# Selective scan: the last two convolution blocks on TensorE beside the scan's first steps

## The chip, the cores and the metric

The kernel runs on one core of a Trainium2 chip. TensorE (PE) multiplies matrices into PSUM, VectorE (DVE), ScalarE (ACT) and GpSimd (POOL) work element by element, and SyncE (SP) starts the transfers. Each engine works through its own instructions in order and waits on semaphores for the others. The metric is the time of one execution on the device in microseconds (us), as the median of several runs. The profile is one further execution, recorded by the hardware profiler.

## The reference

A batch of 8 images, 64 x 64 positions (L = 4096) with 96 channels, goes through four layers, each with a group norm ahead of it and a residual sum behind it. Layers 0 and 2 are selective-scan blocks, layer 1 is a chunked scan and layer 3 an up- and downsampling with a small network between. The change concerns layers 0 and 2. Such a layer does this, for 192 inner channels and 16 states per channel:

```
xm, z = split(in_proj(x))
u     = silu(conv3x3_depthwise(xm) + conv_b)          # 'SAME' padding, 9 taps per channel
for each of 4 directions k (rows, columns, and both reversed):
    delta, B, C = projections of u;  delta = softplus(delta + bias)
    h[l] = h[l-1] * exp(delta[l] * A) + (delta[l] * u[l]) * B[l]
    y[l] = sum over states of h[l] * C[l]
y  = sum of the 4 directions + D * u
out = out_proj(layernorm(y) * silu(z))
```

## The kernel before

The 192 channels lie as two halves (`hf`) of 96 partitions. `y[96, 2, 4096]` first holds the projected input xm, `u[96, 2, 4096]` the convolved one; the scan's sums then overwrite `y` block by block. A block is 8 rows of the image, 512 positions (`LC`); there are 8 blocks.

`selective_scan` is called for layers 0 and 2 of each of the 8 images, 16 times in all. It has two stages.

The **front** makes u. `conv` (lines 249 to 257) convolves some rows of one half on DVE, one instruction per tap, and applies SiLU on ACT. `conv_block` (642) makes one block on PE: per half nine matmuls with a diagonal matrix of the tap's weights, made on POOL by `diagonals` (259) into a buffer `dg`, all adding up in PSUM (`acc`); `silu_block` (648) brings it through ACT to u. DVE makes blocks 0 to 4 (rows 0 to 40) and PE blocks 5, 6 and 7. Between them `prepare_part` sets off the parts of steps 0 and 1 of the scan. The PSUM pool of `acc` is released at the end of the front, and the buffers `das` of the scan take its place: their memset on line 674 is DVE's first work after the front.

The **scan** has 32 steps (4 directions x 8 blocks), and each has 6 units of 32 channels with all 16 states. The loop on line 682 runs over t = 6 i + n, step i and unit n. For each unit,

- `enter` (526) writes the start states into `db` (ACT),
- `spread` (536) copies the unit's channels of delta * u over the partitions into `pu`, a single PSUM buffer (PE),
- `with_b` (543) multiplies them with B into `db`: on DVE from `pu`, or on POOL for every third unit,
- `decays` (555) makes exp(delta * A) on ACT, two instructions for each of the two buffers `das[p]`, which the scan of the unit before must have left,
- `scan` (569) runs the recurrence on DVE, one instruction for each p,
- `leave` (586) copies the end state (ACT), and then POOL multiplies h with C in place. The product waits for that copy. `h` has 5 buffers.

`total_y` (600) adds up three units over the states on PE into `py`, at n = 3 for the first half and at n = 0 of the next step for the second; ACT copies the sum to y at n = 4 and n = 1 (line 702). `prepare` (441) makes ready step i in seven parts, called at fixed places of the two steps before: matmuls into `pv`, copies and softplus on ACT, the product du on POOL, and transfers on SP's queue to spread rows over the partitions. `py` and `pv` share one PSUM buffer (tag `py`, one buffer).

The order is written out by hand (`tc.manual_schedule()`): each engine's instructions come in the order in which the Python code issues them, and only the waits are put in by the framework. No planner moves anything.

Of the kernel before, what the change touches and what calls it, by code (L numbers as in the profile page):

```python
# [9 lines left out]
F32 = mybir.dt.float32  # L10
AF = mybir.ActivationFunctionType
# [6 lines left out]
DM = 96  # L18
# [4 lines left out]
LC = 512  # L23
# [12 lines left out]
C_CW = C_OUT + 192  # L36
C_CB = C_CW + 18
# [27 lines left out]
def tile_vision_stack(  # L65
# [19 lines left out]
    nc = tc.nc  # L85
# [21 lines left out]
    ident = cst[:, K_ID : K_ID + 128]  # L107
# [34 lines left out]
    with (  # L142
# [6 lines left out]
        for i, (dtw, dtx, w) in enumerate(((dt0, dx0, w0s), (dt2, dx2, w2s))):  # L149
# [10 lines left out]
            for k in range(K):  # L160
                pw = pp.tile([DM, 2, 192], F32, name="pw", bufs=2)
                for hf in range(2):
# [4 lines left out]
                        start=True,  # L167
                        stop=True,
# [68 lines left out]
    def taps(y, rows, hf, acc):  # L237

        at, end = rows
        av = acc.rearrange("p (r c) -> p r c", c=64)  # L240
        xv = y[:, hf, :].rearrange("p (r c) -> p r c", c=64)
        for tap in (4, 0, 1, 2, 3, 5, 6, 7, 8):
            dy, dx = tap // 3 - 1, tap % 3 - 1
            r0, r1 = max(at, -dy), min(end, 64 - dy)
            c0, c1 = max(0, -dx), min(64, 64 - dx)
            src = xv[:, r0 + dy : r1 + dy, c0 + dx : c1 + dx]
            yield tap, src, av[:, r0 - at : r1 - at, c0:c1]

    def conv(w, y, u, rows, hf):
        out = u[:, hf, rows[0] * 64 : rows[1] * 64]  # L250
        for tap, src, dst in taps(y, rows, hf, out):
            cw = w[:, C_CW + hf * 9 + tap : C_CW + hf * 9 + tap + 1]
            if tap == 4:
                nc.vector.tensor_scalar_mul(dst, src, cw)
            else:
                nc.vector.scalar_tensor_tensor(dst, src, cw, dst, ALU.mult, ALU.add)
        silu(w, u, rows, hf, out)
# [7 lines left out]
    def conv_pe(dg, y, j, hf, acc):  # L265
        for tap, src, dst in taps(y, (8 * j, 8 * j + 8), hf, acc):
            nc.tensor.matmul(dst, dg[:, 9 * hf + tap, :], src, start=(tap == 4), stop=(tap == 8))

    def silu(w, u, rows, hf, acc):
        nc.scalar.activation(  # L270
            u[:, hf, rows[0] * 64 : rows[1] * 64],
            acc,
            AF.Silu,
            bias=w[:, C_CB + hf : C_CB + hf + 1],
        )
# [119 lines left out]
    def view(t, wh, at, n):  # L395

        if not wh:
            return t[:, at : at + n]
        return t.rearrange("p (h w) -> p w h", w=64)[:, at // 64 : (at + n) // 64, :]

    def cut(t, wh):

        return t.rearrange("p (w h) -> p w h", h=64) if wh else t

    def selective_scan(w, wdt, a, d, u, y):
# [23 lines left out]
        with (  # L429
# [86 lines left out]
            def groups(t):  # L516

                return t[:, 1:].rearrange("p (g s) -> p g s", s=SEG)[:, :, :LC]
# [67 lines left out]
            def leave(t, more):  # L586
# [10 lines left out]
                    prepare_part(i + 1)  # L597
                nc.gpsimd.tensor_mul(h, h, made[i]["c"])  # L598

            def total_y(i, hf):  # L600

                k, c = steps[i]
                wh = k % 2 == 1
                py = pyp.tile([128, LC], F32, name="py", tag="py")[:DM]
                nc.tensor.matmul(  # L605
                    py,
                    skip[:, hf, :] if k == 0 else ident[:DM, :DM],
                    view((u if k == 0 else y)[:, hf, :], wh, c * LC, LC),
                    start=True,
                    stop=False,  # L610
                )
                hs = [groups(made[i].pop(("h", 3 * hf + q))) for q in range(3)]
                for g in range(NSG):
                    for q in range(3):
                        nc.tensor.matmul(  # L615
                            py[32 * q : 32 * q + 32, :],
                            red,
                            hs[q][:, g, :],
                            start=False,
                            stop=(g == NSG - 1),  # L620
                        )
                return view(y[:, hf, :], wh, c * LC, LC), cut(py, wh)
# [3 lines left out]
            def prepare_part(i):  # L626
                if i < len(steps):
                    if i not in going:
                        going[i] = prepare(i)
                    next(going[i], None)  # L630
# [9 lines left out]
            with tc.tile_pool(name="p_conv", bufs=2, space=PSUM) as pvp:  # L640

                def conv_block(n):
                    acc = pvp.tile([DM, 2, LC], F32, name="acc")
                    for hf in range(2):
                        conv_pe(dg, y, n, hf, acc[:, hf, :])
                    return n, acc

                def silu_block(n, acc):
                    for hf in range(2):
                        silu(w, u, (8 * n, 8 * n + 8), hf, acc[:, hf, :])  # L650

                for hf in range(2):
                    conv(w, y, u, (0, 8), hf)
                for _ in range(5):
                    prepare_part(0)
                blocks = [conv_block(5)]
                conv(w, y, u, (8, 24), 0)
                for _ in range(2):
                    prepare_part(0)
                conv(w, y, u, (8, 24), 1)  # L660
                for _ in range(2):
                    prepare_part(1)
                blocks.append(conv_block(6))
                silu_block(*blocks[0])
                conv(w, y, u, (24, 40), 0)
                blocks.append(conv_block(7))
                silu_block(*blocks[1])
                conv(w, y, u, (24, 40), 1)
                silu_block(*blocks[2])
            with tc.tile_pool(name="p_da", bufs=1, space=PSUM) as pap:  # L670
                das = [pap.tile([128, 2 * SEG + 1], F32, name=f"da{p}") for p in range(2)]
                for da in das:
                    for at in range(3):
                        nc.vector.memset(da[:, at * SEG : at * SEG + 1], 0.0)
                states = {}
                for t in range(3):
                    enter(t)
                spread(0)
                decays(0, 0)
                decays(0, 1)  # L680
                with_b(0)
                for t in range(total + 2):
                    n, i = t % units, t // units
                    ahead = t + 1 < total
                    if n in (0, 3) and ahead:
                        spread(t + 1)
                    elif n in (1, 4) and t + 2 < total:
                        spread(t + 2)
                    if n == 0 and i > 0:
                        sums = total_y(i - 1, 1)  # L690
                    elif n == 3:
                        sums = total_y(i, 0)
                    elif n == 4:
                        prepare_part(i + 2)
                    if t < total:
                        scan(t, 0)
                        if n % 3 == 0 and t + 2 < total:
                            with_b(t + 2)
                    if ahead:
                        decays(t + 1, 0)  # L700
                    if n % 3 == 1 and t > 1:
                        nc.scalar.copy(*sums)
                    elif n == 0:
                        prepare_part(i + 1)
                    elif n == 5:
                        prepare_part(i + 2)
                    if t < total:
                        scan(t, 1)
                        leave(t, n == 3)
                    if t + 3 < total:  # L710
                        enter(t + 3)
                    if ahead:
                        decays(t + 1, 1)
                        if (n + 1) % 3 != 2:
                            with_b(t + 1)
                    if n in (0, 1, 5):
                        prepare_part(i + 1)

    def chunked_scan(w, d, u, y):

# [476 lines left out]
    for b in range(batch):  # L1197
        xd = xp.tile([DM, L], F32, name="xd")
        layers = (
            (w0s, lambda u, y: selective_scan(w0s, wdts[0], a0s, dsum[0], u, y)),  # L1200
            (w1s, lambda u, y: chunked_scan(w1s, dsum[1], u, y)),
            (w2s, lambda u, y: selective_scan(w2s, wdts[1], a2s, dsum[2], u, y)),
        )
        with tc.tile_pool(name="layers", bufs=1) as uyp:
            u = uyp.tile([DM, 2, L], F32, name="u")
            y = uyp.tile([DM, 2, L], F32, name="y")
            stats = uyp.tile([DM, 8, 6], F32, name="stats")
            sbs = [uyp.tile([DM, 2], F32, name=f"sb{n}") for n in range(3)] + [sb3]
            for n in range(4):
                with (  # L1210
# [3 lines left out]
                    if n == 0:  # L1214
                        xs = rp.tile([DM, L], F32, name="xs")
                        with (
# [3 lines left out]
                            src = x[b : b + 1].rearrange("b h w c -> (b h w) c")  # L1220
                            src = src.rearrange("(t p) c -> p t c", p=128)
# [21 lines left out]
        dst = out[b : b + 1].rearrange("b h w c -> (b h) w c").rearrange("h w c -> w h c")  # L1243
# [148 lines left out]
```

## Time and profile before

| | |
|---|---|
| median of 3 runs (lowest to highest) | 29505.22 us (29502.27 to 29553.22) |
| the profiled execution, its own time | 29541.08 us |
| span of the profile, first to last instruction | 29539.3 us |
| busy: PE, DVE, ACT, POOL | 78%, 84%, 56%, 74% |
| scans on DVE (line 577) | 6144, 13728.7 us |
| products with C on POOL (line 598) | 3072, 12749.2 us |
| mean granted TensorE clock | 0.761 |

A line of the costliest groups reads: source line, engine, operation, output <- inputs with their shapes, count | busy time, mean ns of one | idle time of the engine just before these instructions, and what ended most of it. A line of a timeline reads: start, length (us), engine, line, operation, output <- inputs, count of merged instructions, and in brackets the idle time of the engine before it with its releaser. A list of waits has the releaser, the total in us and the number of times.

### The profile page before, as it was taken

How to read it: one execution, taken by the hardware profiler on the slowest of the kernel's cores; microseconds unless marked ns; L12 is line 12 of the kernel's file. 1: busy time of each engine (PE TensorE's matmuls, PEld its weight loads, DVE VectorE, ACT ScalarE, POOL GpSimd, SP SyncE). 2: the span in 40 equal slices, each digit the busy share in tenths (PEclk: the TensorE clock that was granted, in tenths of full speed). 3: DMA queues.
4: the chain of work that ended last, by engine and by line, in shares of the span. 5: the costliest groups of instructions: out<-in, count | busy, mean ns of one | idle time of the engine just before them, and what ended most of it. 6: DMA issues, size and time to landing. Idle time of an engine off the chain costs nothing. (4 is left out here: it accounts for less than half of the span.)

```text
span 29539.3 us, 279023 instructions
## 1 busy us (share of the span) xinstructions
PE 23139.1 (78%) x89862; PEld 8801.1 (30%) x89862; DVE 24797.7 (84%) x17920; ACT 16410.5 (56%) x28541; POOL 21775.2 (74%) x8844
## 2 busy tenths in 40 slices
PE   7797877978779787797877978779787797877978
PEld 1151411514115142151421514215141151412414
DVE  9979699796897968979689796897979979699796
ACT  5546455464554645546455464554655546455564
POOL 8859488594885958859588495884958859587594
PEclk7787777877778777787777877778777787777877
DMA  5415254152541525415254152541525415254152
GB/s 124 103 38 133 66 122 102 39 133 65 121 103 39 132 67 120 104 39 131 67 118 105 38 132 68 118 105 38 132 68 122 102 38 132 67 122 102 43 131 65
DMA packets 1509730, 2727.51 MB, mean 92 GB/s; under 512 B 306584, under 2 KB 314104, under 8 KB 1503664
## 3 DMA queue, kind: packets, MB, share of 16 engines
q1 hardware_dynamic: 1491632, 2703.38, 39.2%
q8 instruction: 720, 11.80, 0.2%
q10 hardware_dynamic: 16640, 6.29, 0.1%
q14 instruction: 738, 6.05, 0.1%
HBM read 2325.26 MB, written 383.45 MB: 92 GB/s over the span
## 5 line engine op out<-in xcount | busy, mean ns | idle before, releaser
L577 DVE TENSOR_TENSOR_SCAN h<-da,db 128x1026 f32<-128x1026 f32 x6144 | 13728.7, 2280 | 505.4 <-PE py L615 170.7
L598 POOL TENSOR_TENSOR h<-h,c 128x2048 f32<-128x2048 f32 x3072 | 12749.2, 4178 | 143.2 <-ACT state L593 140.8
L541 PE MATMUL pu<-du,cst 32*128 32x512 f32 x4096 | 3238.8, 881 | 3528.1 <-DVE db L547 3493.8
L562 ACT ACTIVATE da<-dx,a0s 128x512 f32<-128x512 f32 x6144 | 4235.0, 690 | 2593.9 <-DVE h L577 2431.0
L562 ACT ACTIVATE da<-dx,a2s 128x512 f32<-128x512 f32 x6144 | 4234.9, 690 | 2593.2 <-DVE h L577 2428.1
L615 PE MATMUL py<-h,cst 128*32 128x512 f32 x24576 | 5404.1, 810 | 66.4 <-POOL h L598 66.4
L547 POOL TENSOR_TENSOR db<-du,b 128x2048 f32<-128x2048 f32 x1024 | 4653.5, 4544 | 583.9 <-ACT db L533 583.9
L547 DVE TENSOR_TENSOR db<-pu,b 128x2048 f32<-128x2048 f32 x2048 | 4637.5, 2264 | 6.7 <-issue 6.7
L615 PEld LDWEIGHTS py<-h,cst 128*32 128x32 f32 x24576 | 1177.9, 144 | 4956.0 <-issue 4505.2
L541 PEld LDWEIGHTS pu<-du,cst 32*128 32x128 f32 x4096 | 801.6, 243 | 5545.6 <-DVE db L547 4001.4
L463 PE MATMUL pv<-u,wk 96*128 96x512 f32 x2048 | 1766.6, 1004 | 751.1 <-ACT raw L459 751.1
L227 POOL TENSOR_SCALAR xn<-xs,sb 96x512 f32<-96x512 f32 x192 | 217.1, 1136 | 2773.4 <-DVE sb L207 2642.4
L454 PE MATMUL pv<-u,wk 96*96 96x512 f32 x2048 | 1486.2, 855 | 522.0 <-ACT state L593 252.1
L605 PE MATMUL py<-y,cst 96*96 96x512 f32 x1536 | 1551.3, 1108 | 400.5 <-ACT raw L468 361.6
L960 ACT ACTIVATE sg<-sg 128x768 f32<-128x768 f32 x1024 | 819.4, 800 | 1407.4 <-PE sg L944 1407.4
L506 POOL TENSOR_TENSOR du<-raw,u 96x512 f32<-96x512 f32 x1024 | 1443.9, 1434 | 0.0
L992 DVE TENSOR_TENSOR wt<-wt,cbm 128x768 f32<-128x768 f32 x1024 | 1022.3, 1004 | 496.6 <-ACT wt L961 496.4
L593 ACT COPY state<-h 128x4 f32<-128x4 f32 x3072 | 604.5, 197 | 1164.6 <-DVE h L577 1164.6
L1154 DVE SCALAR_TENSOR_TENSOR f<-p,w3bs,f 128x512 f32<-128x512 f32 x768 | 576.4, 750 | 719.6 <-ACT f L1147 692.8
L914 POOL TENSOR_TENSOR ce<-ec,cr 96x512 f32<-96x512 f32 x256 | 406.5, 1588 | 975.5 <-ACT ec L912 971.1
L891 POOL TENSOR_TENSOR rr<-lr,cc 128x768 f32<-128x768 f32 x256 | 375.9, 1468 | 1001.6 <-ACT lr L889 822.8
L463 PEld LDWEIGHTS pv<-u,wk 96*128 96x128 f32 x2048 | 534.3, 289 | 1910.2 <-ACT raw L459 1435.1
(207 smaller groups left out, 31983.9 us busy)
## 6 DMA issues: line engine op xcount, KB each, us to landing
dx<-dd SPq DMA_DIRECT2D x4096, 192.0 KB
b<-bcd SPq DMA_DIRECT2D x2048, 256.0 KB
c<-bcd SPq DMA_DIRECT2D x2048, 256.0 KB
du<-dud SPq DMA_DIRECT2D x2048, 128.0 KB
dd<-raw SPq DMA_DIRECT2D x1024, 192.0 KB
dud<-du SPq DMA_DIRECT2D x512, 128.0 KB
xd<-xs SPq DMA_DIRECT2D x256, 192.0 KB
xs<-xd SPq DMA_DIRECT2D x128, 384.0 KB
```

What stands on the lines that cost most here:

```text
L454: nc.tensor.matmul(pv[:DM], weights[k][:, hi, 128:], uv[hi], start=(hi == 0), stop=(hi == 1))
L463: nc.tensor.matmul(pv, weights[k][:, hi, :128], uv[hi], start=(hi == 0), stop=(hi == 1))
L506: nc.gpsimd.tensor_mul(cut(du[:, hf, :], wh), cut(delta[hf], wh), uv[hf])
L541: nc.tensor.matmul(pu, sel[rows, :], m["du"][rows, n // 3, :], start=True, stop=True)
L547: (nc.gpsimd if pool else nc.vector).tensor_mul(groups(m["db", n]), (m["du2"][:, n // 3, :] if pool else m["pu"]) .unsqueeze(1) .to_broadc ...
L562: nc.scalar.activation(dst[:, g, :LC], made[i]["dx"][n // 3][:, n % 3, :], AF.Exp, scale=av4[:, k, n, gs : gs + 1],)
L577: nc.vector.tensor_tensor_scan(made[i]["h", n][:, at][:, way], das[p][:, rev : 2 * SEG + rev][:, way], made[i]["db", n][:, at][:, way], 0. ...
L598: nc.gpsimd.tensor_mul(h, h, made[i]["c"])
L605: nc.tensor.matmul(py, skip[:, hf, :] if k == 0 else ident[:DM, :DM], view((u if k == 0 else y)[:, hf, :], wh, c * LC, LC), start=True, st ...
L615: nc.tensor.matmul(py[32 * q : 32 * q + 32, :], red, hs[q][:, g, :], start=False, stop=(g == NSG - 1),)
L960: nc.scalar.activation(sg, sg, AF.Abs)
L992: nc.vector.tensor_mul(it["wt"], it["wt"], m["cbm"][:, j : j + 1, :].to_broadcast([128, RK, Q]),)
```

## The change

The front makes only blocks 0 to 5: DVE blocks 0 to 3 (rows 0 to 32) and PE blocks 4 and 5. Blocks 6 and 7 are made inside the scan's loop, by `conv_piece`, in four pieces each, two per half. A piece makes its tap diagonals on ACT, five or four of them, from the identity with a scale per partition, into `some`; PE multiplies them with the rows of y into `acc`, which has the tag `py` and so takes the one buffer of `py` and `pv`; ACT copies `acc` to u. The second piece of a half begins with the identity times what the first left in u. With the last piece of a block, ACT applies SiLU with the bias to both halves in place.

`late` says when: at the very end of iteration t = (i, n), behind all that the iteration issued. Block 6 has its pieces at n = 2 of steps 0, 1, 2 and 3, block 7 at n = 1 of steps 1, 2 and 3 and at n = 2 of step 4. Step 6, the first that reads block 6, has its first matmuls issued at n = 4 of step 4.

```diff
+            def conv_piece(n, piece):
+
+                hf, second = piece // 2, piece % 2 == 1
+                acc = pyp.tile([128, LC], F32, name="acc", tag="py")[:DM]
+                out = u[:, hf, n * LC : n * LC + LC]
+                if second:
+                    nc.tensor.matmul(acc, ident[:DM, :DM], out, start=True, stop=False)
+                mine = list(taps(y, (8 * n, 8 * n + 8), hf, acc))
+                mine = mine[5:] if second else mine[:5]
+                some = tp.tile([DM, 5, DM], F32, name="some")
+                for at, (tap, _, _) in enumerate(mine):
+                    col = C_CW + 9 * hf + tap
+                    nc.scalar.activation(
+                        some[:, at, :], ident[:DM, :DM], AF.Copy, scale=w[:, col : col + 1]
+                    )
+                for at, (tap, src, dst) in enumerate(mine):
+                    nc.tensor.matmul(
+                        dst,
+                        some[:, at, :],
+                        src,
+                        start=(tap == 4),
+                        stop=(at == len(mine) - 1),
+                    )
+                nc.scalar.copy(out, acc)
+                if piece == 3:
+                    for hf in range(2):
+                        at = slice(n * LC, n * LC + LC)
+                        nc.scalar.activation(
+                            u[:, hf, at],
+                            u[:, hf, at],
+                            AF.Silu,
+                            bias=w[:, C_CB + hf : C_CB + hf + 1],
+                        )
+
...
-                blocks = [conv_block(5)]
+                blocks = [conv_block(4)]
                 conv(w, y, u, (8, 24), 0)
...
-                blocks.append(conv_block(6))
+                blocks.append(conv_block(5))
                 silu_block(*blocks[0])
-                conv(w, y, u, (24, 40), 0)
-                blocks.append(conv_block(7))
+                conv(w, y, u, (24, 32), 0)
                 silu_block(*blocks[1])
-                conv(w, y, u, (24, 40), 1)
-                silu_block(*blocks[2])
+                conv(w, y, u, (24, 32), 1)
+
+
+            late = {(n, 2): (6, n) for n in range(4)}
+            late.update({(1 + n, 1 if n < 3 else 2): (7, n) for n in range(4)})
+
...
                     if n in (0, 1, 5):
                         prepare_part(i + 1)
+                    if (i, n) in late:
+                        conv_piece(*late[i, n])
```

## The prediction

> **What bounds the kernel now.** I read the page's costliest groups first, to see which engines could set the time of the two selective-scan layers (16 runs of `selective_scan`, 32 steps of 6 units each):
>
> ```profile
> L577 DVE TENSOR_TENSOR_SCAN h<-da,db 128x1026 f32<-128x1026 f32 x6144 | 13728.7, 2280 | 505.4 <-PE py L615 170.7
> L598 POOL TENSOR_TENSOR h<-h,c 128x2048 f32<-128x2048 f32 x3072 | 12749.2, 4178 | 143.2 <-ACT state L593 140.8
> L547 POOL TENSOR_TENSOR db<-du,b 128x2048 f32<-128x2048 f32 x1024 | 4653.5, 4544 | 583.9 <-ACT db L533 583.9
> L547 DVE TENSOR_TENSOR db<-pu,b 128x2048 f32<-128x2048 f32 x2048 | 4637.5, 2264 | 6.7 <-issue 6.7
> ```
>
> DVE has 13728.7 + 4637.5 = 18366 us there. POOL has 12749.2 + 4653.5, and 1443.9 for du (L506): 18847. Both hardly idle once the scan runs: POOL's 583.9 is 16 waits of some 37 us for the front, before the first unit. So the scan is paced by POOL and DVE together, and the front (convolutions, before the first scan) is extra. Next, line 674, the first DVE work after the front, and its waits:
>
> ```profile
>   ACT u L270: 328.3, 16
> ```
>
> All 16 fronts end with DVE idle, 20.5 us each, for a SiLU. The timelines of ACT, PE and DVE in the first front say which:
>
> ```profile
> 92.86 31.72 PE L267 MATMUL acc<-y,c 96*96 96x512 f32 x72
> ...
> 109.97 1.26 ACT L270 ACTIVATE u<-acc,w0s 96x512 f32<-96x512 f32 x2 [16.48 <-PE acc L267]
> ...
> 111.12 1.14 ACT L270 ACTIVATE u<-u,w0s 96x1024 f32<-96x1024 f32 x1
> ...
> 124.62 1.26 ACT L270 ACTIVATE u<-acc,w0s 96x512 f32<-96x512 f32 x2 [12.36 <-PE acc L267]
> ...
> 125.95 0.62 DVE L674 MEMSET da<- 128x1 f32 x6 [22.49 <-ACT u L270]
> ```
>
> 72 matmul instructions are blocks 6 and 7 (18 taps each, two instructions per tap). PE sets the end of the front: DVE's convolutions were over at 103.5.
>
> Last, one step of the scan, here step 1, n = 1 to 4, from the timelines of ACT, PE, DVE and POOL:
>
> ```profile
> 177.69 1.41 ACT L562 ACTIVATE da<-dx,a0s 128x512 f32<-128x512 f32 x2
> 179.51 1.42 ACT L562 ACTIVATE da<-dx,a0s 128x512 f32<-128x512 f32 x2 [0.41 <-DVE h L577]
> 181.69 0.20 ACT L593 COPY state<-h 128x4 f32<-128x4 f32 x1 [0.77 <-DVE h L577]
> ...
> 181.89 1.41 ACT L562 ACTIVATE da<-dx,a0s 128x512 f32<-128x512 f32 x2
> 186.27 1.42 ACT L562 ACTIVATE da<-dx,a0s 128x512 f32<-128x512 f32 x2 [2.97 <-DVE h L577]
> ```
> ```profile
> 176.76 1.12 PE L541 MATMUL pu<-du,cst 32*128 32x512 f32 x2
> 183.89 2.07 PE L541 MATMUL pu<-du,cst 32*128 32x512 f32 x2 [6.01 <-DVE db L547]
> ```
> ```profile
> 177.18 4.48 DVE L577 TENSOR_TENSOR_SCAN h<-da,db 128x1026 f32<-128x1026 f32 x2 [0.34 <-ACT da L562]
> 181.57 2.26 DVE L547 TENSOR_TENSOR db<-pu,b 128x2048 f32<-128x2048 f32 x1
> 183.94 4.48 DVE L577 TENSOR_TENSOR_SCAN h<-da,db 128x1026 f32<-128x1026 f32 x2
> 188.34 2.27 DVE L547 TENSOR_TENSOR db<-pu,b 128x2048 f32<-128x2048 f32 x1
> 190.71 8.85 DVE L577 TENSOR_TENSOR_SCAN h<-da,db 128x1026 f32<-128x1026 f32 x4
> ```
> ```profile
> 173.70 12.48 POOL L598 TENSOR_TENSOR h<-h,c 128x2048 f32<-128x2048 f32 x3
> ```
>
> The reader is to see three things. DVE goes without a gap but for 0.34 us. POOL's third product here (unit n = 2) starts at about 173.70 + 2 x 4.15 = 182.0, while its scan ended at 181.66 and its state copy at 181.89: POOL's lead at n = 2 is 0.1 to 0.3 us. So a DVE delay goes almost whole into the end, and POOL, busy without a break, cannot win it back. ACT's idle time (2.97 us and the like) comes in pieces of at most 3 us, each ended by DVE.
>
> [...] the pair on L541 takes 1.12 us right after the y sums (176.76) and 2.07 after 6.01 idle (183.89); in the first front matmuls started at 89.29 came 0.85 us apart until 96.18 and then 0.425. I go by the trace: about six slow instructions, then fast. [...] Silu and Exp do change tables in the trace, 1.28 us a load.
>
> **The change, part by part.** Times are those of the first front and of step 1.
>
> *Front.* PE makes one block less. The chain to the first of the two late blocks (diagonals on POOL to 81.77, skip, du to 88.62, raw copy, pv matmuls, 92.86) stays, so the last SiLU pair is now the one at 109.97, followed on ACT by the SiLU of the shorter last DVE part (96x512, 0.72 us): 111.12 + 0.72 = 111.84, against 124.62 + 1.26 = 125.88. The decays of unit 0 come 14.0 us earlier, and DVE (memset, first product) 14.7; the first scan waits for the later of them. In the second front the SiLU pairs start at 2117.21 and 2131.87: 14.66 - 0.62 = 14.0 again. DVE's own saving (8 rows less in each of two calls, some 10 us) lies before PE's end and is worth nothing. The transfers for step 0 were issued by 94.2, so nothing of them is late at 112. Gain 14.0 x 16 = 224 us.
>
> *A piece in the scan.* 5 diagonals on ACT: ACTIVATE 128x512 with a scale pointer takes 690 ns; less 416 elements at the slope of the copies (578 ns at 512, 197 at 4: 0.75 ns each) it is about 0.36 us; only the first delays PE. Then 5 products (or 4 and the identity), 10 instructions: 4.25 us at full rate, 6 x 0.85 + 4 x 0.425 = 6.8 after an idle. Then ACT's copy out of acc, 0.58, for which ACT, in order, stands still. Behind it wait the next decays and the state copy that POOL needs; behind the matmuls on PE waits the next spread (pu), for which DVE's product waits. PSUM's one py buffer is free then (the sums copy ended at 177.6).
>
> *At n = 1 (three times).* Start 179.10; matmuls from 179.55, PE still warm: to 183.8; copy to 184.5; decays to 185.85; the scan that began at 183.94 begins at 185.95: 2.0 us.
>
> *At n = 2 after one at n = 1.* ACT: decays to 185.85, state, enter, decays to 187.56; matmuls from 188.0, PE idle since 183.8, so slow: to 194.8; spread to 195.9; DVE's product 196.0 to 198.36; scan 198.4 against 190.71. Both pieces together 7.7.
>
> *At n = 2 of step 0.* Decays end at 147.06, matmuls 147.55 to 154.35 (PE had been idle), spread to 155.4, product at 155.5 against 152.09: 3.4.
>
> *Last pieces.* Two SiLU (1.35) and two table loads (2 x 1.29) on ACT before the next decays. Step 3: copy ends 195.5, then 196.8, 198.15, 199.45, decays 200.85, scan 200.95: 10.2 with its n = 1 piece. Step 4, alone: matmuls 183.75 to 190.55, copy 191.2, then 5.4 as before: scan at 196.7, 6.0.
>
> Sum per layer 3.4 + 7.7 + 7.7 + 10.2 + 6.0 = 35.0; POOL's lead hides 0.3. Net 34.7 - 14.0 = 20.7, times 16 = +331. The profiled execution took 29541.1 us (span 29539.3); it goes to 29872. Put on the median of the runs, 29505.2, which is 36 below it: **29836**.
>
> Bounds of the sum: four slow instructions instead of six and cheaper diagonals take 5.6 off a layer (+240 in all); eight slow ones, and four also at n = 1, add 9.4 (+480).
>
> **Rivals.**
> 1. *All pieces hidden.* ACT is busy 56%, PE's weight loads and matmuls leave gaps at n = 1 and 2. Then only the front counts: 29505 - 224 = 29281, faster. The place is the decays behind a piece; it decides where the mean stall of the 8 pieces is under 14.0 / 8 = 1.75 us. For it: ACT waits 4859 us for scans. Against: the gaps are 3 us, a piece holds ACT for over 5.
> 2. *PE stays warm.* With all matmuls at 0.425 the same chains give 1.0, 5.2, 5.2, 7.7 and 3.5: 22.6, net 8.3 after the lead, +132: 29637. Against: idle times of 4 to 9 us before four of the five starts, and 2.07 after 6.01.
> 3. *Copy reloads tables.* Up to 2.57 more per piece, about 16 per layer: +587, 30092.
> 4. *The front does not get shorter*, since something else ends there: +555, 30060. Against: DVE, POOL and the transfers end by 104.
>
> **How the numbers follow.** Main case 0.68 (own range 29740 to 29990), warm PE 0.12, hidden 0.08, reload or a dearer piece at n = 1 0.08, front not shorter 0.02, pieces and front cancelling 0.02. Slower 0.90, within 0.2% (59 us, about what a measurement can tell from none) 0.02, faster 0.08. The range leaves out the hidden case and the reload: 29600 to 30060.
>
> **What would show it.** Right: the SiLU before line 674's memset ends some 14 us earlier after the front's start (DVE's wait there shrinks less, to some 17 us each, since DVE is done 10 earlier too); in steps 0 to 4 an out copy on ACT waits for acc 4 to 7 us; DVE waits for pu or decays after each piece, 35 us per layer; POOL idles as much in these steps; steps from 5 on unchanged at 36.2 us. Wrong: POOL has no new idle (rival 1), matmuls of a piece in about 4.3 us at n = 2 (rival 2), table loads before the diagonals (rival 3), or the steps after the pieces run shorter than 36.2 and win time back.

## The result, and the profile after

The changed kernel takes 29669.87 us (median of 4 runs, 29645.07 to 29740.89) against 29511.15 for the kernel before (median of 4 runs beside it): 1.0056 times as long, 95% interval 1.0044 to 1.0068. That is +159 us. The forecast was +331, with a range that began 95 us above the old median, so the side and the range held and the size was twice too large. The main case's own range, 29740 to 29990, missed the result by 70 us; the stated range took it in because it reached down to the warm-PE rival.

The costliest groups of the page after, the same four lines that the prediction shows of before:

```profile
L577 DVE TENSOR_TENSOR_SCAN h<-da,db 128x1026 f32<-128x1026 f32 x6144 | 13728.5, 2280 | 686.8 <-ACT da L562 282.1
L598 POOL TENSOR_TENSOR h<-h,c 128x2048 f32<-128x2048 f32 x3072 | 12747.9, 4176 | 580.2 <-ACT state L593 353.5
...
L547 POOL TENSOR_TENSOR db<-du,b 128x2048 f32<-128x2048 f32 x1024 | 4654.2, 4545 | 327.6 <-ACT db L533 327.6
L547 DVE TENSOR_TENSOR db<-pu,b 128x2048 f32<-128x2048 f32 x2048 | 4638.3, 2265 | 299.6 <-PE pu L541 293.0
```

Busy times are the same as before. What changed is the idle time ahead of the instructions. DVE's scans and products waited 505.4 + 6.7 = 512.1 us before and 686.8 + 299.6 = 986.4 now: 474 more, 29.6 per layer. The new releasers are PE's spread (`pu`) and ACT's decays. POOL's products with C idle 580.2 instead of 143.2. Only the 583.9 that POOL waited for the fronts fell, to 327.6.

The list of waits of line 711, the memset that is DVE's first work after the front (line 674 before):

```profile
  ACT u L270: 166.2, 16
```

It was 328.3. DVE's own convolutions also end earlier, so this difference is not yet the gain of the front. That is in the timeline of the first front after (start, length, engine, line, operation, in brackets the idle time before it):

```profile
82.15 3.19 POOL L506 TENSOR_TENSOR du<-raw,u 96x512 f32<-96x512 f32 x2
86.01 1.98 PE L463 MATMUL pv<-u,wk 96*128 96x512 f32 x4 [1.36 <-ACT raw L459]
87.83 15.45 PE L267 MATMUL acc<-y,c 96*96 96x512 f32 x36
103.32 1.26 ACT L270 ACTIVATE u<-acc,w0s 96x512 f32<-96x512 f32 x2 [14.28 <-PE acc L267]
104.47 0.71 ACT L270 ACTIVATE u<-u,w0s 96x512 f32<-96x512 f32 x1
104.65 0.62 DVE L711 MEMSET da<- 128x1 f32 x6 [9.69 <-ACT u L270]
```

36 instructions of one block stand where 72 stood. The order is the forecast one: the SiLU pair of the last PE block, then that of DVE's last part. But the pair starts at 103.32, not at 109.97: the chain ahead of it is faster too (du 3.19 us and pv 1.98, both shown for before further down).

Step 1 after, n = 1 to 4, from the timelines of ACT, PE, DVE and POOL:

```profile
162.25 1.42 ACT L612 ACTIVATE some<-cst,w0s 96x96 f32<-96x96 f32 x5
168.89 0.58 ACT L623 COPY u<-acc 96x512 f32<-96x512 f32 x1 [5.22 <-PE acc L616]
169.37 1.41 ACT L562 ACTIVATE da<-dx,a0s 128x512 f32<-128x512 f32 x2
170.72 0.18 ACT L593 COPY state<-h 128x4 f32<-128x4 f32 x1
...
170.90 1.41 ACT L562 ACTIVATE da<-dx,a0s 128x512 f32<-128x512 f32 x2
172.24 1.16 ACT L612 ACTIVATE some<-cst,w0s 96x96 f32<-96x96 f32 x4
178.02 0.58 ACT L623 COPY u<-acc 96x512 f32<-96x512 f32 x1 [4.62 <-PE acc L616]
178.50 1.41 ACT L562 ACTIVATE da<-dx,a0s 128x512 f32<-128x512 f32 x2
```
```profile
162.66 6.19 PE L616 MATMUL acc<-y,some 96*96 96x512 f32 x10 [1.93 <-ACT some L612]
169.52 1.10 PE L606 MATMUL acc<-u,cst 96*96 96x512 f32 x2 [0.67 <-ACT u L623]
172.65 5.33 PE L616 MATMUL acc<-y,some 96*96 96x504 f32 x8 [2.03 <-ACT some L612]
177.91 1.12 PE L541 MATMUL pu<-du,cst 32*128 32x512 f32 x2
```
```profile
160.39 4.48 DVE L577 TENSOR_TENSOR_SCAN h<-da,db 128x1026 f32<-128x1026 f32 x2 [0.34 <-ACT da L562]
164.79 2.26 DVE L547 TENSOR_TENSOR db<-pu,b 128x2048 f32<-128x2048 f32 x1
170.82 4.48 DVE L577 TENSOR_TENSOR_SCAN h<-da,db 128x1026 f32<-128x1026 f32 x2 [3.77 <-ACT da L562]
179.07 2.29 DVE L547 TENSOR_TENSOR db<-pu,b 128x2048 f32<-128x2048 f32 x1 [3.78 <-PE pu L541]
181.47 8.85 DVE L577 TENSOR_TENSOR_SCAN h<-da,db 128x1026 f32<-128x1026 f32 x4
```
```profile
160.98 4.18 POOL L598 TENSOR_TENSOR h<-h,c 128x2048 f32<-128x2048 f32 x1 [1.31 <-ACT state L593]
171.03 4.17 POOL L598 TENSOR_TENSOR h<-h,c 128x2048 f32<-128x2048 f32 x1 [5.87 <-issue]
```

The piece at n = 1 holds ACT from 163.7 to 168.89. The decays of the next unit stand behind that copy, and DVE waits 3.77 us for them. The piece at n = 2 holds PE until 177.9. The spread stands behind it, and DVE waits 3.78 us for `pu`. POOL stood idle for 5.87 us before its product at 171.03, right behind the state copy of 170.72, and never catches up. (Its 1.31 at 160.98 comes ahead of this step's pieces.)

The stages of a selective-scan layer, worked out from the starts and ends in each trace, mean over the 16 layers, in us. "Front" runs from the group norm's last DVE instruction (line 207) to the first scan, "steps 0 to 4" from there to the first scan of step 5, "layer" from the same start to POOL's last product.

| kernel | median of runs (n) | ratio to before, 95% | front | steps 0 to 4 | layer |
|---|---|---|---|---|---|
| before | 29511.15 (4) | | 89.19 | 181.88 | 1261.18 |
| after | 29669.87 (4) | 1.0056 (1.0044 to 1.0068) | 70.25 | 211.97 | 1272.06 |
| e1: fronts only | 29215.97 (4) | 0.9896 (0.9879 to 0.9912) | 70.12 | 181.92 | 1242.36 |
| e2: pieces only | 30030.07 (4) | 1.0170 (1.0155 to 1.0185) | 89.37 | 212.30 | 1291.60 |
| e3: DVE's four blocks, PE's three | 29466.62 (14) | 0.9983 (0.9975 to 0.9991) | 84.64 | 182.15 | 1256.91 |
| e3b: DVE's five, PE's two | 29307.93 (4) | 0.9935 (0.9920 to 0.9950) | 75.80 | 182.00 | 1248.09 |
| e5: copy out later | 29497.36 (12) | 1.0002 (0.9994 to 1.0011) | 70.44 | 200.01 | 1260.16 |
| e6: no SiLU | 29610.31 (4) | 1.0039 (1.0024 to 1.0054) | 70.16 | 206.14 | 1265.87 |
| e7: identity waits | 29765.97 (4) | 1.0092 (1.0077 to 1.0107) | 70.53 | 216.09 | 1276.05 |
| e4: whole halves at the y sums | 29246.64 (4) | 0.9905 (0.9890 to 0.9919) | 70.08 | 181.94 | 1242.12 |

Each ratio is against runs of before beside it on the same chip: median 29514.78 for e1, e2, e3 and e4, 29493.26 for e3b, e5, e6 and e7. The front gained 18.9 us and steps 0 to 4 lost 30.1. The layer is 10.9 longer, 16 x 10.9 = 174 us, where the timed runs say 159. The rest of a layer didn't move: from step 5 on a step takes 36.58 us in the mean in both (36.24 to 37.6, so the prediction's 36.2 is the shortest), so nothing is won back. The spans of the two profiled executions differ by only 104 us. Single executions scatter that much in the stretches outside these two layers (9290 to 9367 us over the traces used here), which is why the rows above are compared by stages and by the timed medians.

### The profile page after: what moved, and what is told of

It is laid out like the page before. It is cut to its first block, busy times and chain, and to the rows that moved or that the text cites. A ratio compares the mean times of both kernels' runs of the same rounds, so it can differ in the third digit from the quotient of the medians.

```text
span 29643.3 us, 281263 instructions
## 1 busy us (share of the span) xinstructions
PE 23429.5 (79%) x90566; PEld 8868.0 (30%) x90566; DVE 24663.0 (83%) x17920; ACT 16716.4 (56%) x29341; POOL 21729.0 (73%) x8844
## 5 line engine op out<-in xcount | busy, mean ns | idle before, releaser
L577 DVE TENSOR_TENSOR_SCAN h<-da,db 128x1026 f32<-128x1026 f32 x6144 | 13728.5, 2280 | 686.8 <-ACT da L562 282.1
L598 POOL TENSOR_TENSOR h<-h,c 128x2048 f32<-128x2048 f32 x3072 | 12747.9, 4176 | 580.2 <-ACT state L593 353.5
L541 PE MATMUL pu<-du,cst 32*128 32x512 f32 x4096 | 3178.1, 865 | 2960.7 <-DVE db L547 2937.3
L649 PE MATMUL py<-h,cst 128*32 128x512 f32 x24576 | 5286.4, 794 | 61.3 <-POOL h L598 61.3
L547 POOL TENSOR_TENSOR db<-du,b 128x2048 f32<-128x2048 f32 x1024 | 4654.2, 4545 | 327.6 <-ACT db L533 327.6
L547 DVE TENSOR_TENSOR db<-pu,b 128x2048 f32<-128x2048 f32 x2048 | 4638.3, 2265 | 299.6 <-PE pu L541 293.0
L454 PE MATMUL pv<-u,wk 96*96 96x512 f32 x2048 | 1564.0, 896 | 640.7 <-ACT y L739 337.3
```

Source lines behind the costliest of these rows:

```text
L454: nc.tensor.matmul(pv[:DM], weights[k][:, hi, 128:], uv[hi], start=(hi == 0), stop=(hi == 1))
L541: nc.tensor.matmul(pu, sel[rows, :], m["du"][rows, n // 3, :], start=True, stop=True)
L547: (nc.gpsimd if pool else nc.vector).tensor_mul(groups(m["db", n]), (m["du2"][:, n // 3, :] if pool else m["pu"]) .unsqueeze(1) .to_broadc ...
L577: nc.vector.tensor_tensor_scan(made[i]["h", n][:, at][:, way], das[p][:, rev : 2 * SEG + rev][:, way], made[i]["db", n][:, at][:, way], 0. ...
L649: nc.tensor.matmul(py[32 * q : 32 * q + 32, :], red, hs[q][:, g, :], start=False, stop=(g == NSG - 1),)
```

## The experiments

**The two halves of the change by themselves.** e1 leaves the pieces out:

```diff
                 blocks.append(conv_block(5))
+                nc.gpsimd.memset(u[:, :, 6 * LC :], 0.0)
                 silu_block(*blocks[0])
...
-                    if (i, n) in late:
-                        conv_piece(*late[i, n])
```

> The shorter front alone: blocks 0 to 5 as in the changed kernel, no pieces in the scan; blocks 6 and 7 of u are left at zero (a POOL memset where POOL idles), so two convolution blocks are left out. By the prediction's sum the front saves 14.0 us per layer: about 29511 - 224 = 29287. By the trace of the changed kernel it saves 18.9 per layer (group norm's end to first scan 70.3 us against 89.2): about 29209, with steps 0 to 4 at 181.9 us as before. If the shorter front itself disturbed the first steps (transfers not landed), steps 0 to 4 would be longer than 182.

e2 keeps the pieces and gives the front back its old work:

```diff
-                blocks = [conv_block(4)]
+                blocks = [conv_block(5)]
...
-                blocks.append(conv_block(5))
+                blocks.append(conv_block(6))
                 silu_block(*blocks[0])
-                conv(w, y, u, (24, 32), 0)
+                conv(w, y, u, (24, 40), 0)
+                blocks.append(conv_block(7))
                 silu_block(*blocks[1])
-                conv(w, y, u, (24, 32), 1)
+                conv(w, y, u, (24, 40), 1)
+                silu_block(*blocks[2])
```

> The pieces alone: the front of before makes all eight blocks, and the scan makes blocks 6 and 7 once more in the eight pieces, with the same values. If the pieces alone cause the loss and add to the front's gain, steps 0 to 4 take 212 us instead of 182, and the time is about 29511 + 16 x 30.1 = 29993; by the prediction's sum (34.7) it is 30066. If part of the loss came from the shorter front (scan started sooner), it is under 29900.

Measured against the median of before in the same comparison, 29514.78: e1 -299 us, e2 +515. By stages, e1's front is 19.1 shorter and its steps 0 to 4 are untouched (181.92). e2's front is untouched (89.37) and its steps 0 to 4 are 30.4 longer. The two parts don't act on each other: 30.4 - 19.1 = 11.3, the whole change 30.1 - 18.9 = 11.2. (The timed medians add up less well, -299 + 515 = +216 against +159; they hold the scatter outside these layers too.) So both terms of the forecast can be judged alone: it put the front's gain 4.9 us a layer too low and the pieces' loss 4.6 too high, two misses that add up.

**Why the front gains more.** e3 takes from the kernel before only DVE's share of the fifth block, e3b only PE's third block:

```diff
                 blocks.append(conv_block(6))
+                nc.gpsimd.memset(u[:, :, 4 * LC : 5 * LC], 0.0)
                 silu_block(*blocks[0])
-                conv(w, y, u, (24, 40), 0)
+                conv(w, y, u, (24, 32), 0)
                 blocks.append(conv_block(7))
                 silu_block(*blocks[1])
-                conv(w, y, u, (24, 40), 1)
+                conv(w, y, u, (24, 32), 1)
```

> DVE's share alone: DVE makes blocks 0 to 3, PE blocks 5, 6 and 7 as before, no pieces; block 4 of u is left at zero. The prediction held DVE's saving for worth nothing (PE ends the front): 29511, within 0.2%. The rival from the changed trace: with DVE's shorter instructions POOL's chain ahead of PE's last blocks (diagonals, skip, du) ends 3.3 us sooner, PE's gap before the second pv matmuls falls from 3.9 to 1.4 us so that they run at full clock (1.98 for 3.78), and the front gets about 5 us shorter: 29511 - 80 = 29431.

```diff
                 conv(w, y, u, (24, 40), 0)
-                blocks.append(conv_block(7))
+                nc.gpsimd.memset(u[:, :, 7 * LC :], 0.0)
                 silu_block(*blocks[1])
                 conv(w, y, u, (24, 40), 1)
-                silu_block(*blocks[2])
```

> PE's share alone: DVE makes blocks 0 to 4 as before, PE blocks 5 and 6, no pieces; block 7 of u is left at zero. DVE's instructions are those of before up to the end, so POOL's chain and the pv matmuls should be as late as before (first product of PE's second block some 5 us later than in the changed kernel): the front ends with DVE's last SiLU at 111.12 + 1.14 = 112.3 instead of 125.88, 13.6 us per layer: 29515 - 218 = 29297. If one block less on PE were by itself worth the 18.9 us of the changed front, 29213.

e3's front is 84.64, 4.55 us shorter; e3b's is 75.80, 13.4 shorter. The forecast 14.0 was PE's share alone, and it was nearly exact. DVE's share, taken as worth nothing, is the other 4.6 to 5.5. The two together, 17.9, leave 1.0 us of the 18.9. Most of that is seen in e3b: its front ends with the SiLU of DVE's last part, 1.14 us for 96x1024 where the shorter part takes 0.71, and its second stretch of products on PE starts 0.47 later than before's (below). By the timed medians the shares come to -48 and -185 us, together -233 against e1's -299; the stages agree better.

DVE's work itself ended before PE's in every one of these fronts, so its share must act through somebody else. The timelines of POOL, ACT and PE in the first front tell through whom. Before:

```profile
84.38 4.24 POOL L506 TENSOR_TENSOR du<-raw,u 96x512 f32<-96x512 f32 x2
```
```profile
88.65 0.58 ACT L459 COPY raw<-pv 96x512 f32<-96x512 f32 x1 [8.12 <-POOL du L506]
```
```profile
89.29 3.78 PE L463 MATMUL pv<-u,wk 96*128 96x512 f32 x4 [3.88 <-ACT raw L459]
```

e3:

```profile
83.23 3.20 POOL L506 TENSOR_TENSOR du<-raw,u 96x512 f32<-96x512 f32 x2
```
```profile
86.47 0.58 ACT L459 COPY raw<-pv 96x512 f32<-96x512 f32 x1 [5.23 <-POOL du L506]
```
```profile
87.10 1.98 PE L463 MATMUL pv<-u,wk 96*128 96x512 f32 x4 [0.92 <-ACT raw L459]
```

e3b:

```profile
84.51 4.24 POOL L506 TENSOR_TENSOR du<-raw,u 96x512 f32<-96x512 f32 x2
```
```profile
89.42 2.99 PE L463 MATMUL pv<-u,wk 96*128 96x512 f32 x4 [3.84 <-ACT raw L459]
```

In e3 POOL's pair takes 3.20 us instead of 4.24 and starts 1.15 earlier, since the diagonals (24.38 us for 25.39) and the skip matrices (1.57 for 2.63) ahead of it are shorter too. ACT's copy into `raw` waits for the pair, which reads `raw`, and the pv matmuls wait for the copy. So both start 2.2 us earlier (87.10 against 89.29). PE's gap ahead of them is 0.92 instead of 3.88, and the four instructions take 1.98 instead of 3.78: another 1.8. The products behind come 0.42 to 0.43 us apart from the first on, where the first of before came 0.77 to 0.86 apart (until 96.18) and then 0.42 to 0.43. Over the layers the mean gain is 4.55. In e3b the pair's length, its start and PE's gap are as before. Over the 16 fronts PE's second stretch of products starts 53.39 us after the group norm before, 53.86 in e3b, 49.73 in e3 and 49.83 after the change. What POOL's instructions took beside DVE's is taken up in the last section.

**Where the pieces lose: ACT.** e5 moves the copy out of PSUM (and the SiLU) one place on, behind the first pair of the next unit's decays:

```diff
+                held.append((n, piece, out, acc))
+
+            held = []
+
+            def piece_out(n, piece, out, acc):
+
                 nc.scalar.copy(out, acc)
                 if piece == 3:
...
                     if ahead:
                         decays(t + 1, 0)
+                    if held:
+                        piece_out(*held.pop())
```

> The changed kernel with each piece's copy out of acc (and the SiLU) issued one place later: behind the next decays instead of ahead of them. So ACT does not stand still for PE ahead of decays that the scan needs; PE's order is unchanged. If both causes hold as worked out (at n = 1 ACT waiting in order, at n = 2 the spread queued behind the products on PE), the waits at n = 1 go (3.8, 0.9 and 2.2 us in the first layer) and so does about half of the SiLU's 5.3, those at n = 2 stay: steps 0 to 4 at about 203 us instead of 212, 29670 - 144 = 29526. If ACT's wait is the only cause, all goes: about 29220. If PE's queue is the only one, 29670 stays.

Steps 0 to 4 take 200.0 instead of 212.0, and the kernel is level with the one before (1.0002). The groups of its page:

```profile
L577 DVE TENSOR_TENSOR_SCAN h<-da,db 128x1026 f32<-128x1026 f32 x6144 | 13735.4, 2281 | 532.1 <-PE py L655 173.5
...
L547 DVE TENSOR_TENSOR db<-pu,b 128x2048 f32<-128x2048 f32 x2048 | 4640.7, 2266 | 251.1 <-PE pu L541 244.4
```

The scans' idle time is nearly that of before (532.1, was 505.4), so the waits for decays are gone. The products' waits for the spread remain at 251.1 (299.6 after). Of 30.1 us a layer, 12 went with ACT's order: the copy, for which it stood waiting for PE, and the SiLU, ahead of decays that were due. By the idle times about 9.7 us a layer came off the scans' waits and 3.0 off the waits for the spread, so the two causes are not fully separate. The 18 that remain are mainly PE's spread standing behind a piece's products (251.1 / 16 = 15.7).

**The SiLU.** e6 leaves it out for blocks 6 and 7:

```diff
-                if piece == 3:
+                if piece == 4:
```

> The changed kernel without the two SiLU (and their table loads) at the end of the two blocks' pieces: the SiLU and the bias of blocks 6 and 7 are left out. By the prediction's chains they cost 2.5 us in step 3 and 2.6 in step 4; DVE's two new waits for decays there are 2.65 each: 5.2 x 16 = 83 less, 29587. If they were hidden behind the spread, 29670.

Steps 0 to 4 fall by 5.8 us. The timeline of ACT in step 3 of the first layer after, and what DVE waits:

```profile
263.39 0.58 ACT L623 COPY u<-acc 96x512 f32<-96x512 f32 x1 [4.62 <-PE acc L616]
263.99 1.28 ACT L627 ACT_TABLE_LOAD   x1
265.28 1.33 ACT L627 ACTIVATE u<-u,w0s 96x512 f32<-96x512 f32 x2
266.63 1.28 ACT L562 ACT_TABLE_LOAD   x1
267.93 1.41 ACT L562 ACTIVATE da<-dx,a0s 128x512 f32<-128x512 f32 x2
```
```profile
269.38 8.85 DVE L577 TENSOR_TENSOR_SCAN h<-da,db 128x1026 f32<-128x1026 f32 x4 [2.65 <-ACT da L562]
```

Two loads and two SiLU put the decays 4.0 us later, and DVE pays 2.65 of it, as the forecast had it (2.5 and 2.6). In e6 these two waits are gone from DVE and the others are as they were within 0.4 us each. (The 5.8 and e5's 12 overlap, since e5 moves the SiLU as well.)

**The identity product.** In the second piece of a half the first product is the identity with what the first piece left in u. e7 lets it wait for a diagonal like the others, by having ACT copy the identity first:

```diff
-                if second:
-                    nc.tensor.matmul(acc, ident[:DM, :DM], out, start=True, stop=False)
...
+                if second:
+                    nc.scalar.activation(some[:, 4, :], ident[:DM, :DM], AF.Copy)
+                    nc.tensor.matmul(acc, some[:, 4, :], out, start=True, stop=False)
```

> The changed kernel with the identity of each second piece copied by ACT as the first of its diagonals, so that the identity product waits for it, as the prediction's working had it (10 instructions behind the first diagonal in all eight pieces). If the prediction's 35 us per layer was too high because this product runs ahead on PE, before the diagonals, the loss rises towards it, by 3 to 5 us per layer: 29670 + 50 to 80 = 29720 to 29750. If the size was off for another reason (the clock, the diagonals), it stays at 29670 within 0.2%.

The timeline of PE, second piece of step 1, in e7:

```profile
170.17 1.10 PE L610 MATMUL acc<-u,some 96*96 96x512 f32 x2 [3.71 <-ACT some L609]
171.10 5.25 PE L617 MATMUL acc<-y,some 96*96 96x504 f32 x8
```

All ten instructions stand in a row behind ACT and take 6.2 us. After the change the pair on the identity ran at 169.52, while ACT was still at the decays, and only eight (5.33 us) came behind the diagonals. e7's steps 0 to 4 are 4.1 us longer than after's, 66 us over the layers, within the forecast 50 to 80 (the timed medians, which were not taken side by side, are 96 apart). Its loss there, 216.1 - 181.9 = 34.2, is close to the forecast 35.0.

**The same work elsewhere.** e4 makes one whole half at a time: nine diagonals on ACT a step ahead, the 18 products on PE right behind the copy of the y sums at n = 1, and at the end of n = 2 one SiLU straight from PSUM. To make room for the nine diagonals, one weight of layer 3 is loaded in each image instead of once.

```diff
...
+            def half_sum(n, hf):
+                acc = pyp.tile([128, LC], F32, name="acc", tag="py")[:DM]
+                for at, (tap, src, dst) in enumerate(taps(y, (8 * n, 8 * n + 8), hf, acc)):
+                    nc.tensor.matmul(
+                        dst, halves["taps"][:, at, :], src, start=(tap == 4), stop=(tap == 8)
+                    )
+                halves["acc"] = acc
+            def half_out(n, hf):
+                silu(w, u, (8 * n, 8 * n + 8), hf, halves["acc"])
...
+            late = {1: (6, 0), 2: (6, 1), 3: (7, 0), 4: (7, 1)}
...
                         nc.scalar.copy(*sums)
+                        if n == 1 and i in late:
+                            half_sum(*late[i])
...
+                    if n == 3 and i + 1 in late:
+                        half_taps(*late[i + 1])
+                    if n == 2 and i in late:
+                        half_out(*late[i])
```

> The same late blocks, placed elsewhere: half a block (9 taps) per step at n = 1 of steps 1 to 4, its matmuls issued right behind the sums copy of n = 1, in PE's idle time ahead of the next spread; the diagonals made one step earlier at the end of n = 3, where ACT idles; SiLU straight from acc at the end of n = 2, where ACT idles too. The 9 diagonals need room, so w3as is loaded in the last layer instead of at the start. If the loss comes from where the pieces stand (ACT waiting in order for PE, the spread queued behind the products), the front's gain stays nearly whole: 16 to 19 us per layer, 29210 to 29260. If the work itself costs (the PE clock, ACT's or PE's load), about half of it is lost: 29350 or more.

It takes 29246.64 us, 0.9905 of before, and steps 0 to 4 take 181.94, as before. Step 1 of the first layer, PE, ACT and DVE:

```profile
156.81 1.12 PE L540 MATMUL pu<-du,cst 32*128 32x512 f32 x2
157.86 7.89 PE L613 MATMUL acc<-y,some 96*96 96x512 f32 x18
165.68 1.12 PE L540 MATMUL pu<-du,cst 32*128 32x512 f32 x2
```
```profile
163.14 1.28 ACT L269 ACT_TABLE_LOAD   x1
165.79 0.68 ACT L269 ACTIVATE u<-acc,w0s 96x512 f32<-96x512 f32 x1 [1.36 <-PE acc L613]
166.49 1.28 ACT L561 ACT_TABLE_LOAD   x1
167.78 1.42 ACT L561 ACTIVATE da<-dx,a0s 128x512 f32<-128x512 f32 x2
```
```profile
163.77 4.48 DVE L576 TENSOR_TENSOR_SCAN h<-da,db 128x1026 f32<-128x1026 f32 x2
168.17 2.27 DVE L546 TENSOR_TENSOR db<-pu,b 128x2048 f32<-128x2048 f32 x1
```

PE idled 6.01 us there before the change, between the spread for n = 1 and the next (177.9 to 183.9). The 18 products follow the y sums and a spread without a gap and come 0.44 us apart (7.89 / 18), and they are over at 165.7, before DVE's product of 168.17 needs its spread. ACT waits 1.36 us, within what it would have waited for DVE. The layer takes 1242.1 us, as in e1, which doesn't make the two blocks at all; the timed medians of the two are 31 us apart, and e4 loads that weight more often (whether that is the reason was not tried). Within these two layers the work of blocks 6 and 7 costs nothing here. e4 moves the products, the diagonals and the SiLU at once, and it has no identity products and no copy of a half sum, so it doesn't tell which of these moves is needed. It does show that the shared PSUM buffer is no reason of its own: its `acc` takes the one buffer of `py` and `pv` too.

## Why the prediction was right about the side and too high

Predicted: front -14.0, steps 0 to 4 +34.7, net +20.7 a layer. Measured: -18.9, +30.1, +11.2. The two misses come to 9.5 us a layer, 152 of the 172 us between forecast and measured difference.

*Front.* The step that failed is "DVE's own saving [...] lies before PE's end and is worth nothing". It looked at DVE's end, which indeed came early enough. It overlooked that POOL's instructions took longer beside DVE's longer ones (du's pair 4.24 us before, 3.20 in e3), and POOL's du is on the very chain that the prediction listed: "(diagonals on POOL to 81.77, skip, du to 88.62, raw copy, pv matmuls, 92.86) stays". It didn't stay; it ended at 87.83. The other step, one block less on PE and SiLU pairs that change places, held: 14.0 against e3b's 13.4. The check named beforehand, DVE's wait at the memset shrinking "to some 17 us", came out at 166.2 / 16 = 10.4, with DVE done 9.0 us earlier. That alone would have told that the front's end had moved further than forecast.

*Pieces.* The step that failed is "Then 5 products (or 4 and the identity), 10 instructions". DVE's waits behind each piece, mean us a layer, without the SiLU's 2.65 in steps 3 and 4:

| piece | instructions behind diagonals | forecast | after | e7 |
|---|---|---|---|---|
| step 0, n = 2 | 10 | 3.4 | 3.44 | 2.95 |
| step 1, n = 1 | 10 | 2.0 | 2.98 | 2.39 |
| step 1, n = 2 | 8 | 5.7 | 3.78 | 4.85 |
| step 2, n = 1 | 8 | 2.0 | 0.89 | 2.67 |
| step 2, n = 2 | 10 | 5.7 | 5.18 | 5.57 |
| step 3, n = 1 | 10 | 2.0 | 2.49 | 2.29 |
| step 3, n = 2 | 8 | 5.7 | 3.78 | 5.29 |
| step 4, n = 2 | 8 | 3.4 | 2.13 | 2.30 |

The four pieces with ten instructions come to 14.1, forecast 13.1. The four with eight, second pieces all, come to 10.6, forecast 16.8: their identity product needs none of the piece's diagonals and ran ahead of them. e7 takes that away and brings these four to 15.1. Part of e7's agreement with the forecast total is compensation: its three pieces at n = 1 cost 7.4, forecast 6.0, and its five at n = 2 cost 21.0, forecast 23.9.

*The other terms held, but for PE's pace at n = 1.* Ten instructions after an idle of 9.2 us (step 0) take 7.1 us in the mean (6.30 to 7.95), and after one of 3.8 (step 2) 6.7, against 6.8. At n = 1 they take 5.34 in step 1 and 4.81 in step 3 (4.49 to 6.19), so PE was not always at the 0.425 us an instruction there that the 4.25 had (in step 1 of the first layer its granted clock was 0.68 from 162.66 to 168.00). The SiLU costs 2.65 in each of steps 3 and 4, against 2.5 and 2.6. A diagonal takes 0.359 us, against about 0.36 (690 less 416 x 0.75 ns would have been 0.38). No table load lies on line 612, which has 576 diagonals; that rules out the third rival; the low weight that the forecast gave it was the author's estimate, with no run behind it. The causes were the ones named (decays behind ACT's copy, the spread behind PE's products), and so was their end: POOL "cannot win it back".

*The rivals.* "All pieces hidden" falls for this placing: the mean stall is 30.1 / 8 = 3.8 us, over the 1.75 from which it would decide. e4 shows that the work itself can be hidden, from other places. "PE stays warm" gave 29637, the number nearest to the result, but not by its mechanism: the products behind diagonals took 4.8 to 7.1 us in the mean in seven of the eight places, where 0.425 us an instruction makes 3.4 to 4.25, and its front was the forecast one. "The front does not get shorter" falls by e1.

What stays open is how much of the loss is PE's pace and how much the order. The products behind diagonals took 13.2 us a layer longer than at 0.425 us an instruction (from the means of the eight places), which is the most that the pace can be worth; no run holds the order and changes the pace alone.

## What to carry to other kernels

Work moved under a busy stage cost here what it put ahead of others in in-order queues, not its busy time: the same 36 tap products and 36 diagonals a layer cost 30 us with the copy out ahead of the decays and the products ahead of the spread, 18 with that copy one place later, and nothing with the products right behind the y sums, where they came 0.44 us apart and PE would idle next, and the diagonals a step ahead. Before placing such work, list on each engine the next instruction that somebody waits for, and put the work behind it. And when an engine that isn't the last is given less to do, follow whom its instructions hold up before its saving is called worthless.

## What the runs showed of the hardware that was not expected

In the front POOL's and DVE's instructions took longer side by side. POOL's element-wise instruction on 96x512 (line 506) takes 1.27 us in the mean in the scan's steps of the same row order, without DVE's convolutions beside it (1.54 in the column orders). In the front it takes 1.6 beside DVE's 96x504 and 96x512 instructions (0.75 us each), and 2.1 beside its 96x1008 and 96x1024 ones (1.3 us each). DVE's instructions were longer as well: the two that overlap POOL's pair take 2.15 and 2.08 us before (1.27 to 1.28 without it) and 1.63 each after the change (0.74 to 0.75). Of DVE's two last parts in the kernel before, the first has POOL's pair beside it, the second nothing of POOL's:

```profile
80.14 12.16 DVE L256 SCALAR_TENSOR_TENSOR u<-y,w0s,u 96x1008 f32<-96x1008 f32 x8
93.00 10.47 DVE L256 SCALAR_TENSOR_TENSOR u<-y,w0s,u 96x1008 f32<-96x1008 f32 x8
```

The single instructions' ends show how. Before, they are DVE 85.32, POOL 86.44, DVE 87.50, POOL 88.62, DVE 89.68: each comes 1.06 or 1.12 us behind the other engine's last. In e3 they are DVE 83.65, POOL 84.77, DVE 85.31, POOL 86.44, DVE 86.98: POOL's come 1.12 behind DVE's, DVE's 0.54 behind POOL's. After the change they stand at the same distances (DVE 82.56, POOL 83.68, DVE 84.22, POOL 85.34, DVE 85.88). These times fit one of the two working at a time while POOL's pair runs, with the pair lasting two turns of its own, one whole DVE instruction and the rest of another: 2.24 + 1.06 + 0.94 = 4.24 before, 2.25 + 0.54 + 0.42 = 3.21 in e3. DVE is busy for 4.10 of the pair's 4.24 us before and for 3.12 of 3.19 after the change, so the pair's length went with the length of DVE's instructions, not with how much DVE had to do. That the two took turns is the author's reading of these times; no run changed DVE's length with its work held equal.

PE's pace after short gaps was worth more than expected: four pv instructions take 1.98 us behind a gap of 0.92 (e3) or 1.36 (after the change, at a granted clock of 1.00), and 3.78 (before, at 0.50) or 2.99 (e3b) behind one of about 3.85. But shorter gaps are followed by slow products too. In the first front of e3 four pv instructions take 3.60 us behind a gap of 2.75, and the next four 3.78 behind one of 0.67. The 2.03 us gap in step 1 after the change is followed by eight instructions in 5.33 us, slower than the 3.32 that eight take at n = 1 of step 2 behind a gap of 0.59 to 0.70, though PE had been busy for 7.3 of the 8.0 us before the gap; all 32 pieces with this gap (n = 2 of steps 1 and 3) take the same 5.33. Nor do they start slow: in step 1 the first three starts are followed by the next after 0.42 to 0.50 us, the four behind them after 0.69 to 0.85, and the granted clock was 0.87 from 172.65 to 174.69 and 0.55 from there to 177.90. So the length of the gap alone did not tell PE's pace behind it, and the slow products came some instructions after it.
